# Two attention layers with routed and ternary feed-forward blocks on one core: attention loops issued in plan order, routing in eleven slot steps, LayerNorm roots and layer 1's normalization on GpSimd

## The chip, the cores and the metric

The kernel runs on one core of a Trainium2 chip. The metric is device microseconds (us) of one execution; lower is better. A core has TensorE (PE: matmuls, with weight loads, PEld, beside them), VectorE (DVE), ScalarE (ACT), GpSimd (POOL) and SyncE (SP, which issues most of the transfers here).

## The reference, cut to what matters

Eight sequences of 112 tokens and 256 features pass through two layers. Each block adds its result to x.

```python
x = x + xattn0(layernorm(x), ctx)      # 16 heads of 16, context of 375, biases
x = x + moe(layernorm(x))              # 8 experts of 256 -> 1024 -> 256, exact gelu, top 2
x = x + xattn1(layernorm(x), ctx, mask)
x = x + ffn(layernorm(x))              # ternary weights, 8-bit activations, depthwise conv, silu

def layernorm(x, eps=1e-5):
    return (x - mean(x)) / sqrt(var(x) + eps)
# routing: distances in a ball between x @ Wp + bp and 8 centroids,
# the two nearest experts, weights by softmax over -distance
```

## The kernel before, in words

All arithmetic on tokens is float32. x lies in SBUF as eight tiles of 112x256 (`xs`).

**Attention** (`attention(layer, ...)`, L479) works on one sequence ("batch" b) at a time and is laid out as a pipeline by a written plan. `add(slot, place, step, *args)` puts steps into the list `plan` (from L677); the loop at L741 calls them sorted by slot, then place, with ties in the order of adding. A batch starts every four slots, n = 4b. Its steps are: `norm` (normalize, two PE transposes t_n, ACT copy), `key` in two halves (t_k, evacuated by ACT), `value` (t_v, evacuated by DVE), `query` (t_q, scaled by DVE), then for the four head groups g `scores` (PE sc; DVE takes the row maximum, in layer 1 with the mask added), `lower` (transposes of the maxima, t_top; DVE adds them to the query as a 17th row), `turned` (transposed scores less the maximum, t_p; in layer 1 four DVE mask adds; two ACT exponentials), `weighted` (PE po), and at the end `finish_o` (ACT copy, PE t_o, DVE division), `finish_t` (PE t_oT, ACT copy) and `project` (PE t_out, DVE adds to x, then `ln_stats` for the next block).

PSUM holds three "pair" buffers of two banks, which sc (two of them), t_p (two), t_k and t_v (one each) take in turn; one "misc" bank, which t_n, t_q, t_top, t_o, t_oT, t_out, t_rn and t_xh take in turn; and one bank for po and the small products. A product waits until the engine that reads its buffer's last content is done.

`ln_stats` (L204) takes mean and variance, adds 1e-5 and calls `rsqrt` (L185): an integer first guess and three Newton steps, nine VectorE operations that wait for each other nearly all. `ln_apply` (L215) normalizes on VectorE.

In layer 0 the plan also holds the **routing** of the batches that are done (`Router`, L246, called by `route`), in eight steps from slot n+13 on: normalize and transpose (r_n, t_rn), products with Wp (t_xh), `centre` (products with the centroids and a DVE root), `distance`, two `pick`s, `place` (rank of each token by a product with a triangle, row numbers, two scatters of the normalized rows into `tok` in DRAM by GpSimd), and `weigh` (the two shares, a root of two columns). After it `further` works out which extra expert tiles there are. The ternary weights of the last block are made here as well (`ternary`, slots 8 to 19), and layer 1's keys and values of batches 0 and 1 (slots 31 to 45).

**Experts** (L756 on): 21 tiles of 128 rows are fetched from `tok`, pass through their expert with weights that come by transfers, and are written to `ysc` in DRAM. Layer 1's attention begins with `combine` (L506): two gathers of rows of `ysc` by GpSimd, two DVE multiply-adds into x, `ln_stats`. The **last block** quantizes and runs on bf16.

What an engine runs in which order is not given by the program's order: the framework's scheduler lists instructions by their priority (their place in the program) and by when it expects their inputs, engine by engine, and may put a later instruction ahead of an earlier one.

## Time and profile before

| | |
|---|---|
| median of the runs | 797.11 us (795.2 to 800.27) |
| the profiled execution, its own time | 795.12 us |
| its span, from the first to the last instruction | 793.4 us |
| mean granted TensorE clock | 0.841 |
| busy: PE, PEld, DVE, ACT, POOL | 670.2, 483.3, 462.1, 240.9, 43.3 us |
| attention 0 | 0 to 294 us |
| experts | 294 to 457 us |
| attention 1 | 457 to 700 us |
| last block | 700 to 793 us |

In the rows of slices each digit is the busy share of one fortieth of the span in tenths; the row PEclk has the granted clock in the same way. PE's records are modelled, so a busy PE includes products that run at half the clock and some of their waits. The table by windows gives, after the window's length, the busy time of each engine with the number of its instructions, then the clock, the share of the DMA engines and GB/s. The chain of waits leads back from the last instruction to what released it each time: start, length, engine, what it wrote, its line. A line of the timeline has start, length, engine, line, operation, output and input with shape.

### The profile page before, as it was taken

What the parts mean: (1) busy time and instruction counts of PE and PEld (TensorE: products, weight loads), DVE (VectorE), ACT (ScalarE), POOL (GpSimd) and SP (SyncE); (2) the same over time, 40 slices, a digit from 0 to 9 for tenths busy, and PEclk for the clock granted to TensorE, in tenths of its full rate; (3) what the DMA queues carried; (4) which work ended last, traced back from release to release, by engine and by line L of the source; (5) the groups of instructions that cost most, each with busy time, mean ns of one, the idle gap of its engine ahead of it and who ended that gap; (6) DMA issues with size and microseconds to landing.
All of it is one profiled execution on the core that took longest, in us unless ns stands there. A gap on an engine that the chain in (4) does not pass through costs nothing.

```text
span 793.4 us, 15060 instructions
## 1 busy us (share of the span) xinstructions
PE 670.2 (84%) x5906; PEld 483.3 (61%) x5906; DVE 462.1 (58%) x1664; ACT 240.9 (30%) x476; POOL 43.3 (5%) x83
## 2 busy tenths in 40 slices
PE   4999998999989819999999968999999989845143
PEld 2666666666656519998999844566666656621033
DVE  8853767766844760111111148759887785569975
ACT  1123342323233204434334310133433322317300
POOL 4000000100000110000000061000000000000000
PEclk9998999989777959999999975579999985556558
DMA  9999101002000115988899420000000000000001
GB/s 309 366 344 321 62 2 54 14 13 68 14 12 8 31 45 206 332 287 327 331 351 344 169 82 19 1 2 1 2 2 2 2 2 1 1 1 0 0 11 35
DMA packets 37074, 82.73 MB, mean 104 GB/s; under 512 B 3228, under 2 KB 29196, under 8 KB 31628
## 3 DMA queue, kind: packets, MB, share of 16 engines
q1 hardware_dynamic: 34092, 76.25, 27.2%
q0 software_dynamic: 1536, 3.67, 1.5%
q10 hardware_dynamic: 1376, 1.87, 0.7%
q8 instruction: 46, 0.75, 0.4%
q14 instruction: 24, 0.20, 0.1%
HBM read 61.59 MB, written 20.19 MB: 103 GB/s over the span
## 4 chain that ended last, share of the span: by engine, by line
PE 68%; DVE 20%; DMA 5%; issue 4%; ACT 3%; POOL 0%; another core or an unknown queue 0%; POOLq 0%; DVEq 0%; ACTq 0%; SPq 0%
PE t_k L229 10%; PE t_h L799 10%; PE t_y L810 9%; PE t_p L617 8%; PE sc L584 7%; PE po L639 6%; PE t_q L534 4%; PE t_v L236 4%; DMA tok<-rn,at 2%; DVE a L198 2%; PE t_out L672 2%; DVE am L924 2%; PE t_o L651 1%; DVE top L587 1%; PE t_y L942 1%
## 5 line engine op out<-in xcount | busy, mean ns | idle before, releaser
L229 PE MATMUL t_k<-ctx,wk 128*128 128x375 f32 x256 | 100.5, 538 | 4.0 <-DMA ctx<-in_ctxT_dram 3.2
L799 PE MATMUL t_h<-tnT,we 128*128 128x128 f32 x672 | 91.4, 280 | 0.6 <-DMA we<-in_WA_dram 0.4
L799 PEld LDWEIGHTS t_h<-tnT,we 128*128 128x128 f32 x672 | 87.1, 193 | 7.5 <-ACT hT L803 1.6
L584 PE MATMUL sc<-k,q 16*112 16x375 f32 x512 | 88.0, 593 | 4.3 <-DVE pT L627 3.2
L803 ACT ACTIVATE hT<-t_h,we 128x128 f32<-128x128 f32 x168 | 61.4, 368 | 91.3 <-PE t_h L799 85.7
L617 PE MATMUL t_p<-qa,k 17*125 17x112 f32 x1536 | 81.9, 323 | 2.4 <-DVE top L587 1.5
L810 PE MATMUL t_y<-we,hT 128*128 128x256 f32 x336 | 82.8, 380 | 0.0
L629 ACT ACTIVATE pT<-pT 125x672 f32<-125x672 f32 x64 | 48.8, 763 | 107.7 <-DVE pT L627 105.5
L617 PEld LDWEIGHTS t_p<-qa,k 17*125 17x125 f32 x1536 | 65.0, 215 | 21.2 <-issue 14.8
L587 DVE TENSOR_REDUCE top<-sc 112x2 f32<-112x750 f32 x64 | 57.9, 935 | 27.2 <-PE sc L584 27.2
L229 PEld LDWEIGHTS t_k<-ctx,wk 128*128 128x128 f32 x256 | 51.1, 211 | 37.1 <-issue 9.7
L627 DVE TENSOR_TENSOR pT<-t_p,maskT 125x336 f32<-125x336 f32 x128 | 56.6, 500 | 24.9 <-PE t_p L617 24.9
L639 PE MATMUL po<-pT,v 125*32 125x112 f32 x1536 | 65.9, 299 | 6.1 <-ACT pT L629 3.7
L629 ACT ACTIVATE pT<-t_p 125x672 f32<-125x672 f32 x64 | 43.3, 728 | 90.7 <-PE t_p L617 90.7
L594 DVE CUSTOM_DVE_ANT_0 sm<-sc,mask 112x375 f32<-112x375 f32 x128 | 63.1, 543 | 9.9 <-PE sc L584 9.9
L639 PEld LDWEIGHTS po<-pT,v 125*32 125x32 f32 x1536 | 43.4, 124 | 31.4 <-ACT pT L629 13.3
L810 PEld LDWEIGHTS t_y<-we,hT 128*128 128x128 f32 x336 | 59.1, 191 | 5.5
L788 DVE COPY tnT<-t_tn 128x256 f32<-128x256 f32 x21 | 8.9, 425 | 77.2 <-PE t_tn L786 70.6
L812 DVE TENSOR_TENSOR y<-t_y,we 128x256 f32<-128x256 f32 x21 | 8.9, 425 | 68.9 <-PE t_y L810 63.9
L584 PEld LDWEIGHTS sc<-k,q 16*112 16x112 f32 x512 | 29.4, 192 | 30.9 <-issue 19.7
L236 PE MATMUL t_v<-wv,ctx 128*125 128x256 f32 x192 | 45.9, 387 | 0.3 <-ACT k L557 0.3
L534 PEld LDWEIGHTS t_q<-nT,wq 128*128 128x128 f32 x256 | 36.2, 225 | 7.5 <-DVE qa L607 3.7
(207 smaller groups left out, 780.6 us busy)
## 6 DMA issues: line engine op xcount, KB each, us to landing
we<-in_WB_dram SPq DMA_DIRECT2D x21, 1152.0 KB, 8.2
we<-in_WA_dram SPq DMA_DIRECT2D x21, 1028.0 KB, 6.5
tok<-zero SPq DMA_DIRECT2D x8, 896.0 KB, 9.7
ysc<-zero SPq DMA_DIRECT2D x8, 896.0 KB, 10.8
ctx<-in_ctxT_dram SPq DMA_DIRECT2D x8, 375.0 KB, 6.5
tn<-tok SPq DMA_DIRECT2D x21, 128.0 KB, 7.4
ysc<-y SPq DMA_DIRECT2D x21, 128.0 KB, 3.3
we<-in_w1T_dram SPq DMA_DIRECT2D x1, 1024.0 KB, 9.4
```

What stands on the lines that cost most here:

```text
L229: nc.tensor.matmul(t, wts[layer]["k"][:, c, g * 128 : (g + 1) * 128], ctx_t[b][:, c, :], start=(c == 0), stop=(c == 1),)
L236: nc.tensor.matmul(t, ctx_t[b][:, c, i * KC : (i + 1) * KC], wts[layer]["v"][:, c, :], start=(c == 0), stop=(c == 1),)
L534: nc.tensor.matmul(t[:, g, :], wts[layer]["q"][:, c, g * 128 : (g + 1) * 128], nT[:, c, :], start=(c == 0), stop=(c == 1),)
L584: nc.tensor.matmul(ts[j // 2][:S, j % 2, :SK], q[r, g, :], k[r, g, :], start=True, stop=True)
L587: nc.vector.tensor_reduce(top[:, g, 2 * m : 2 * m + 2, A : A + 1], ts[m][:S, :, :SK], AX.X, ALU.max, negate=True,)
L594: nc.vector.tensor_tensor_reduce(out=sm, in0=ts[m][:S, i, :SK], in1=mask_t, scale=-1.0, scalar=3.0e38, op0=ALU.add, op1=ALU.min, accum_out ...
L617: nc.tensor.matmul(ts[j // 2][:KC, j % 2, c * S : (c + 1) * S], k[r, g, c * KC : (c + 1) * KC], qa[r, g, :], start=True, stop=True,)
L629: nc.scalar.activation(pT, src, AF.Exp)
L639: nc.tensor.matmul(po[32 * j : 32 * j + 32, g, :], v[:, c, 4 * g + j, :], pTs[j // 2][:, j % 2, c * S : (c + 1) * S], start=(c == 0), stop ...
L799: nc.tensor.matmul(ph[:, i, :], w1[:, c, f * 128 : (f + 1) * 128], nt[:, c, :], start=(c == 0), stop=(c == 1),)
L803: nc.scalar.activation(hT[:, f, :], ph[:, i, :], AF.Gelu, bias=b1[:, f : f + 1])
L810: nc.tensor.matmul(py, hT[:, f, :], w2[:, f, :], start=(f == 0), stop=(f == NF - 1))
```

## The change

The attention plans run inside `tc.manual_schedule` for PE, DVE, ACT and POOL: these four engines take the steps' instructions in the plan's order. SP isn't among them. The steps are divided further and moved:

- `combine`'s gathers become a step `gather`, three slots earlier; `combine` itself moves from place 0 to 5.
- `norm` is split: normalize at n-6, transposes (`norm_t`) at n-5. In layer 1, for b > 0, GpSimd normalizes.
- `finish_o`'s ACT copy becomes `finish_c` at n+9, place 8; `finish_o`, `finish_t` and `project` move from place 1 to 2.5, behind `weighted`.
- key, value and layer 1's early keys and values change places, the last three of them slots too.
- routing has eleven steps: the transposes, the root of `centre` (now `scale`) and the rank product of `place` (now `rank`) stand alone. Its normalized rows have three buffers in place of two.
- LayerNorm's root is two GpSimd operations, an add and a power of -0.5. The roots of the routing stay on VectorE.

```diff
+    minus_half = const([128, 1], "mhalf")
+    nc.gpsimd.memset(minus_half, -0.5)
...
         nc.vector.bn_aggr(mv, st)
-        nc.vector.tensor_scalar_add(mv[:, 1:2], mv[:, 1:2], 1e-5)
         rs = sp.tile([S, 1], F32, tag=f"rs{b}", name="rs")
-        rsqrt(mv[:, 1:2], rs, 1, "ln")
+        nc.gpsimd.tensor_scalar_add(rs, mv[:, 1:2], 1e-5)
+        nc.gpsimd.tensor_tensor(rs, rs, minus_half[:S], ALU.pow)
...
-    def ln_apply(dst, b, stats):
+    def ln_apply(dst, b, stats, eng=None):
         mv, rs = stats
-        nc.vector.tensor_scalar(dst, xs[b], mv[:, 0:1], rs, ALU.subtract, ALU.mult)
+        (eng or nc.vector).tensor_scalar(dst, xs[b], mv[:, 0:1], rs, ALU.subtract, ALU.mult)
...
-            g, r = tmp("g", E + 1), tmp("r", 1)
+            return t
+
+        def scale(self, t):
+            g, r = self.tmp("g", E + 1), self.tmp("r", 1)
             nc.vector.tensor_copy(g, t)
             self.ball_scale(g[:, E : E + 1], r, 1, "x")
             return g, r
...
+        def rank(self, b):
+
+            ind = self.ind
             t = self.small("t_rank")[:S, :E]
             nc.tensor.matmul(t, below[:S, :S], ind, start=True, stop=(b == 0))
             if b > 0:
                 nc.tensor.matmul(t, ones[:S, :S], count[(b - 1) % 2][:S], start=False, stop=True)
+            if b == 0:
+                nc.vector.tensor_copy(count[0][:S], ind)
+            else:
+                nc.vector.tensor_add(count[b % 2][:S], count[(b - 1) % 2][:S], ind)
+            return t
...
-            def combine(b):
-
+            def gather(b):
+
+                st[b]["y"] = []
                 for k in range(2):
                     y = ap3.tile([S, D], F32, tag=f"yg{k}", name="yg")
                     nc.gpsimd.indirect_dma_start(
...
+                    st[b]["y"].append(y)
+
+            def combine(b):
+                for k, y in enumerate(st[b].pop("y")):
                     nc.vector.scalar_tensor_tensor(xs[b], y, share[b][:, k : k + 1], xs[b], ALU.mult, ALU.add)
                 stats[b] = ln_stats(b)
 
             def norm(b):
                 n = ap.tile([S, D], F32, tag="n", name="n")
-                ln_apply(n, b, stats.pop(b))
+                ln_apply(n, b, stats.pop(b), nc.gpsimd if layer == 1 and b > 0 else nc.vector)
...
+            def finish_c(b):
+                st[b]["ou"] = ap.tile([128, G, S], F32, tag="ou", name="ou")
+                nc.scalar.copy(st[b]["ou"], st[b].pop("po"))
+
...
                 if layer == 1:
-                    add(n - 8, 0, combine, b)
-                add(n - 5, 6, norm, b)
+                    add(n - 11, 0, gather, b)
+                    add(n - 8, 5, combine, b)
+                add(n - 6, 6, norm, b)
+                add(n - 5, 6, norm_t, b)
                 if layer == 0 or b >= AHEAD:
 
                     ahead = layer == 1 and b == 2
-                    add(-7 if ahead else n - 4, 4, key, layer, b, 0)
-                    add(-7 if ahead else n - 3, 5, key, layer, b, 1)
-                    add(-7 if ahead else n - 2, 6, value, layer, b)
+                    add(-10 if ahead else n - 4, 4, key, layer, b, 0)
+                    add(-9 if ahead else n - 3, 4, key, layer, b, 1)
+                    add(-7 if ahead else n - 2, 4, value, layer, b)
                 add(n - 3, 2, query, b)
                 add(n + 4, 6, lower, b)
-                add(n + 10, 1, finish_o, b)
-                add(n + 11, 1, finish_t, b)
-                add(n + 12, 1, project, b)
+                add(n + 9, 8, finish_c, b)
+                add(n + 10, 2.5, finish_o, b)
+                add(n + 11, 2.5, finish_t, b)
+                add(n + 12, 2.5, project, b)
...
-                        r["n"] = rt.norm(b, stats_next.pop(b))
+                        r["n"] = rt.norm(b, stats_next.pop(b), ap3)
...
-                    for i in range(8):
-                        add(4 * b + 13 + i, 5 if i == 6 else 7, route, b, i)
+                    for i in range(11):
+                        add(4 * b + 13 + i, 7, route, b, i)
...
-                for b, ns in enumerate(((3, 6, 9), (15, 16, 17))):
-                    add(last + ns[0], 4, key, 1, b, 0)
-                    add(last + ns[1], 4, key, 1, b, 1)
-                    add(last + ns[2], 4, value, 1, b)
-
-            for slot, place, step, args in sorted(plan, key=lambda s: s[:2]):
-                step(*args)
-            if layer == 0:
-                res = rt.further()
+                for b, ns in enumerate(((3, 6, 9), (16, 18, 20))):
+                    add(last + ns[0], 8, key, 1, b, 0)
+                    add(last + ns[1], 8, key, 1, b, 1)
+                    add(last + ns[2], 8, value, 1, b)
+
+            ET = mybir.EngineType
+            with tc.manual_schedule(engines={ET.PE, ET.DVE, ET.Activation, ET.Pool}):
+                for slot, place, step, args in sorted(plan, key=lambda s: s[:2]):
+                    step(*args)
+                if layer == 0:
+                    res = rt.further()
```

Steps 0 to 10 of `route` are then: normalize, turn, hyper, centre, scale, distance, pick 0, pick 1, rank, place, weigh.

## The prediction

> **What bounds the kernel now.** I read, in order, the busy slices of the page, the table by windows, the chain of waits, and the timelines of four stretches. The profiled execution took 795.12 us, span 793.4. The page's slices (19.8 us each) show where TensorE (PE) is not full and where its granted clock falls:
>
> ```profile
> PE   4999998999989819999999968999999989845143
> ...
> DVE  8853767766844760111111148759887785569975
> ...
> PEclk9998999989777959999999975579999985556558
> ```
>
> PE is at 8 to 9 tenths in both attention loops, and its clock falls to 5 to 7 tenths in slices 11 to 13, 15, 24 to 27 and 34 to 39, counted from 1. By stage (attention 0, experts, attention 1, last block; columns: length, then PE, weight load, VectorE (DVE), ScalarE (ACT), GpSimd (POOL), clock):
>
> ```profile
> 0.00:294.00 294.00, 253.81 (x2512) 173.11 (x2512) 193.98 (x866) 84.70 (x165) 28.27 (x67) 0.89 0.33 111
> 294.00:457.00 163.00, 159.24 (x1053) 145.95 (x1054) 17.79 (x42) 62.72 (x169) 0.00 (x0) 0.98 0.79 288
> 457.00:700.00 243.00, 223.50 (x2214) 144.36 (x2213) 173.51 (x633) 70.08 (x101) 14.99 (x16) 0.78 0.03 9
> 700.00:793.00 93.00, 33.66 (x130) 19.92 (x129) 76.79 (x123) 23.36 (x41) 0.00 (x0) 0.60 0.03 10
> ```
>
> The experts are untouched. The loops leave 40 and 20 us of PE idle, and run at 0.89 and 0.78 of the clock. In the chain of waits the query product returns once a batch (start, length):
>
> ```profile
> 93.91 1.97 PE t_q L534 x16
> ...
> 121.56 3.60 PE t_q L534 x16
> ...
> 151.75 2.04 PE t_q L534 x16
> ...
> 181.71 2.04 PE t_q L534 x16
> ...
> 526.88 1.97 PE t_q L534 x16
> ...
> 551.07 1.97 PE t_q L534 x16
> ...
> 575.26 1.97 PE t_q L534 x16
> ```
>
> So a batch takes 27.65, 30.2 and 30.0 us in layer 0 while routing joins, but 24.2 us in layer 1 at full clock. The timeline of layer 1 (575 to 600 us) has PE without a gap and already in the plan's order, slot for slot. Issue in the plan's order therefore can't speed up the steady part; what it can change is the fill, the drain, and how VectorE's small operations mix. In a chain of dependent ones each starts 0.195 us after the one before:
>
> ```profile
> 240.11 0.16 DVE L202 SCALAR_TENSOR_TENSOR q<-a,q 112x2 f32<-112x2 f32 x1
> 240.31 0.16 DVE L200 TENSOR_TENSOR a<-q 112x2 f32<-112x2 f32 x1
> 240.50 0.16 DVE L201 SCALAR_TENSOR_TENSOR a<-a,z 112x2 f32<-112x2 f32 x1
> ```
>
> where the timeline at 145.8 to 146.5 us, two chains mixed, has starts 0.065 us apart. The order before mixes chains wherever it can; the plan's order runs one after the other.
>
> [...] during a GpSimd add at 17.22 us (0.73 us) a VectorE L202 took 0.65 us, not 0.15. [...] at 464 us (idle 7 us, then 0.50), but from 660 to 690 us PE is busy 29.2 of 30 us by the records at 0.50, so busy by the records isn't enough.
>
> **The change part by part.** Units: r0 to r3 are the slots 4b to 4b+3 of a batch; durations are from the timelines.
>
> *Start, +4.0.* The preamble and the plan's first slots now keep their order. Before, centroids ran mixed in and the first scores began at 24.08 us, the second query at 29.22. Now the centroid chain (16 dependent operations, about 3.2 us) stands after value 0's three adds (1.1) and batch 1's normalization (0.4), and before the first score reduction; its matmul stands before the first scores. From batch 0's normalization at 12.5 PE has t_n, t_k (5.0 with the starts of now), t_q 2.0, t_k and t_v 2.8 each: values end at about 25.6. Then csq is ready at 27.3, scores at 28, the chain ends at 31.4, the reduction that frees the pair buffer at 32.3; the second query then starts at 33.3.
>
> *Routed slots 13 to 31, +7.2.* Removed: ten root operations per batch from VectorE, mostly mixed into other chains, so worth about 0.1 us each, 1.0 us of a 30 us batch, which PE sets. Moved: the routing steps stand at place 7, behind value's adds and ahead of the next slot's reduction. From the end of a value product VectorE must now do, in order: adds 1.1, norm 0.4, place 0.85, distance (9 x 0.195) 1.75, reductions 1.8, weigh (16 x 0.195, plus) 3.3, pick 1.0, first reduction 0.93: 11.1 us before r0's t_p has its buffer. PE has turn, scores, po, t_oT, t_p, t_n, t_xh, scores, po, t_out: about 7.5. The rest of the batch on PE is t_p, t_k, t_top, t_g, scores, po, t_q, t_p, t_k, rank, scores, po, t_o, t_p, t_v: 18.6 by starts. So 29.8 us at full clock. Before, half-clock spells (142 to 148, 169 to 178 us) cost 1.7 and 3.4, mean 2.5, of its 30.0; I take 1.8 now, since part falls into the stall. 31.6 against 30.0, 4.5 batches.
>
> *Slots 31 to the experts, +2.5.* The order before wandered here: from the scores at 218.57 to batch 7's o at 264.62 it took 46.0 us, with t_p and po split in pieces (235 to 243) and turn waiting for a scatter to free its buffer (1.3 and 1.9 us). With three buffers and whole steps PE has about 33 us at full clock, 38.5 at 0.85 of it: -7.5. Then the drain is VectorE's: slots 38 to 50 hold, in order, two place, two distance, two weigh, five picks, two scales and so on, one chain after the other; by the durations above 33.1 us from o to batch 7's rows. Before, mixed, 264.62 to 288.1 (the cast): 23.4. +9.7, and 0.3 for PE's rank. Batch 1's t_k and t_v (8.4 us on PE), moved to slots 44 to 48, are hidden in this chain; without it they would cost 8.4. The two scatters behind the rows (5.7 us to the first expert load at 293.8) are the same.
>
> *Layer 1's start, -8.4.* The last y is done at 456.04. The gathers land as before (461.64, 462.82). Statistics end at 464.0. The root on GpSimd, add and power, appears nowhere in the trace: at least two memsets of 90 ns, at most two descriptor instructions of 0.95; I take 0.5. Value 2's copy (0.95) covers it up to 465.0. Normalize, transpose, copy, query at half clock: 470.3. Ahead of the query's scaling VectorE has combine 1, whose gathers now stand behind root 0 on GpSimd: issued 464.5 and 465.75, landing 2.85 later; scaling at 470.4. Batch 1's normalization stands on GpSimd behind root 1 and two gathers (2.5) and takes 0.3 (its memset of that size) to 0.73 (its two-input add); I take 0.7: 473.2. PE's transposes wait for it, the scores behind them: 474.0 against 479.78. Then six scores (1.6 at half clock), two queries (3.76), small transposes (2.3): first t_p at 493.7 against 500.64; VectorE is no longer behind, as it has combine 2 and 3 only, not 2 to 5 (1.6 and a 1.9 us root each). Then three slots of t_p, two mask adds, second exp, po: 1.54+1.85+0.8+1.15 = 5.4; the first key product at 511.5 against 519.87. Gathers three slots earlier are worth nothing in later batches: the data waited anyway. At 2 us instead of 0.5 a root would give back 3 us here.
>
> *Layer 1's steady part, +2.6.* Removed: the root's 1.9 us chain, which held the scores of r1 up (1.64 us where 0.90 is work): -0.75. Added: t_out now follows po, which waits for an exp, and no longer fills that wait: +0.75. finish_c's copy stands on ACT behind exp and key's evacuation (0.89+0.53), and po of r2 waits for it: PE has scores (0.83) ahead: +0.65. Four batches. GpSimd's normalization has a slot of slack. SP's queue isn't among the four ordered engines, and its transfers stand where they stood.
>
> *Layer 1's drain, +1.2* (t_o, t_oT, t_out now between po and t_p, one after the other; before, they lay in the waits), *last block, -1.0* (eight chained operations of batch 7).
>
> Sum: 4.0+7.2+2.5-8.4+2.6+1.2-1.0 = +8.1 us: 803.2 for the profiled execution. The median is 1.99 above it: 805.2.
>
> **Rivals.** (1) Faster, by the clock. At reduced clock attention 0 loses (20 to 270 us, window by window) about 25 us of PE time, attention 1 about 42. If even slots without wandering order keep the clock up and half of 67 returns, 8.1-33 gives 772; it decides from 8 us (an eighth), and below 0.99 from 16. For it: the clock falls at 464 with idle PE, and the wandering stretch 210 to 240 has 0.68. Against: 660 to 690 us has no heavy products, which the change leaves so. I would expect a quarter to a half, 772 to 789. (2) Much slower: the stalls of r3 halve the clock in each routed batch (3 us more, 13 in all) and in layer 1's steady part (24.2 us toward 28, 16 in all): 834. For it: spells at 142 and 169 us begin in just these slots. Against: layer 1's scores wait there already, at 1.00. (3) No difference: the steps behave as the order before, since PE's order hardly changes, and start and fill cancel: 797. Against: the serial drain is plain arithmetic. (4) That roots or normalization on GpSimd are not off the path (slow power, waits behind gathers): 3 to 8 us more; a part of my case's range.
>
> **How the numbers follow.** My case 0.47, own range 796 to 820 (root 0.2 to 2 us, half-clock 0 to 3 us a batch, drain mixed by halves); (1) 0.28; (2) 0.15; (3) 0.10. About 1% (789 to 805) is what a measurement of this kernel tells from no change. Slower: 0.28 of my 0.47, and (2): 0.43. Faster: (1) but 0.01: 0.27. Same: 0.19 of mine, 0.01 of (1), and (3): 0.30. The range leaves out 0.1 below, where (1) returns more than a third, and 0.1 above, most of (2): 781 to 832.
>
> **What would show it.** Right: a routed batch near 31 us with DVE the releaser of t_p; place, distance and weigh in unbroken 0.195 us steps; o of batch 7 to its cast near 33 us; layer 1's first t_p about 38 us after the last y (before 44.6); 24.8 us a batch. Wrong: a drain under 27 us, a clock above 0.85 in attention 1, or GpSimd roots above 1 us.

## The result and the profile after

The changed kernel takes 847.69 us (842.58 to 855.38, 4 runs) against 797.59 us before on the same chip: ratio 1.061, 95% interval 1.054 to 1.067. Slower by 6%, well above the forecast of 805.2 and its range. The profiled execution is the slowest of the four: 855.38 us, span 853.7, so its stages add up to 60.3 us more than before, some 10 more than the medians differ. The ratios and intervals in this document leave out executions that took over 1.5% more than the fastest of the same kernel (the profiled one is such a case); the medians hold all of them.

The page's rows of slices, now 21.3 us each:

```profile
PE   3799989889899872999999987999999998645233
...
DVE  4444555565666677010111015767777675359974
...
PEclk9798998796857856999999995579899885556558
```

PE is as full as before or nearly, VectorE a little less busy (449.6 us in place of 462.1), and the clock row has its low digits spread over the whole of attention 0 (slices 2, 8, 10, 12, 13, 15 and 16) instead of a few places. The table by windows at the new borders:

```profile
0.00:341.50 341.50, 276.13 (x2512) 188.68 (x2512) 198.26 (x706) 84.29 (x165) 41.84 (x100) 0.81 0.29 96
341.50:502.00 160.50, 159.11 (x1050) 145.53 (x1050) 17.81 (x42) 62.64 (x169) 0.00 (x0) 0.99 0.79 291
502.00:761.00 259.00, 228.25 (x2216) 146.62 (x2216) 157.36 (x478) 68.95 (x101) 36.70 (x53) 0.74 0.03 9
761.00:853.00 92.00, 32.34 (x128) 19.93 (x128) 76.20 (x113) 23.43 (x41) 0.87 (x2) 0.61 0.04 10
```

Attention 0 takes 47 us longer, at a clock of 0.81 in place of 0.89; attention 1 takes 16 us longer, at 0.74 in place of 0.78. The same products keep PE busy 22 and 5 us longer, which I put down to the lower clock; the rest is idle. The query products in the chain of waits give the batches:

```profile
140.16 1.97 PE t_q L553 x16
...
174.01 1.97 PE t_q L553 x16
...
212.10 1.97 PE t_q L553 x16
...
621.52 1.97 PE t_q L553 x16
...
647.85 1.97 PE t_q L553 x16
```

33.8 and 38.1 us a batch in layer 0 (before 27.7 to 30.2), 26.3 us in layer 1 (28.3 in the batches between; before 24.2).

Cutting each profiled execution at the same events (VectorE's addition of a batch's t_out to x, "out 0" to "out 7"; the first expert's first product; the last y) gives the table that the rest refers to. The three columns on the right are experiments ("last version" is the last one of them).

| us | before | changed | no order by hand | all repairs | last version |
|---|---|---|---|---|---|
| start to out 0 | 88.4 | 103.2 | 88.4 | 91.5 | 92.5 |
| out 0 to 4 (routed batches) | 114.8 | 135.5 | 124.1 | 108.9 | 109.4 |
| out 4 to 7 | 67.6 | 63.1 | 60.7 | 67.2 | 54.8 |
| out 7 to first expert product | 25.3 | 39.8 | 26.5 | 39.1 | 26.6 |
| experts | 159.6 | 160.1 | 160.4 | 160.0 | 159.7 |
| last y to layer 1's out 0 | 88.9 | 86.1 | 88.0 | 86.2 | 83.4 |
| out 0 to 4 | 96.6 | 108.8 | 109.5 | 105.1 | 95.1 |
| out 4 to 7 | 59.7 | 64.4 | 59.0 | 52.9 | 51.8 |
| last block | 92.5 | 92.8 | 91.8 | 93.1 | 92.7 |

Each column is one execution. Some experiments keep the changed kernel's order of instructions in one layer, so that their traces measure that part again: out 0 to 4 took 131.5 to 139.4 us in five traces of layer 0 and 102.0 to 108.8 us in four of layer 1. Both ranges lie above the kernel before, whose own trace has 114.8 and 96.6, but a difference of a few microseconds between two columns can be the execution's.

Three places in the trace show where it goes. **The start**, by the timeline:

```profile
27.75 0.35 DVE L783 TENSOR_SCALAR mask<-mask 112x375 f32<-112x375 f32 x1 [7.10 <-DMA mask<-in_mask_dram]
...
29.32 0.34 DVE L784 TENSOR_SCALAR maskT<-maskT 125x336 f32<-125x336 f32 x1 [1.22 <-DMA maskT<-in_maskT_dram]
...
31.12 0.61 PE L543 MATMUL t_n<-ident,n 112*128 112x112 f32 x2 [6.00 <-DVE csq L270]
...
32.34 1.60 PE L603 MATMUL sc<-k,q 16*112 16x375 f32 x8
```

Two scalings of the masks, which only layer 1 reads and which stand behind attention 0 in the program, are outside the part ordered by hand, and the scheduler put them ahead of value 0's additions. There VectorE waits for the masks' transfers with all of the start behind it; before, the same two ran at 33.79 and 34.06 us, and neither waited. The brackets hold the idle time before an instruction and what ended it.

**A routed batch**, while the scores of batch 5 run, from value's additions to t_p's wait:

```profile
187.06 1.09 DVE L590 TENSOR_TENSOR v<-t_v,rows 125x256 f32<-125x256 f32 x3 [2.33 <-PE t_v L239]
...
188.38 0.16 DVE L382 TENSOR_TENSOR row<-po,first 112x8 f32<-112x8 f32 x1
...
189.69 0.21 DVE L330 SCALAR_TENSOR_TENSOR xn<-g,r 112x1 f32<-112x1 f32 x1
...
191.77 1.78 DVE L606 TENSOR_REDUCE top<-sc 112x2 f32<-112x750 f32 x2
...
192.75 1.60 PE L636 MATMUL t_p<-qa,k 17*125 17x112 f32 x20 [2.63 <-DVE top L606]
```

Between the additions and the reductions VectorE normalizes and does place (188.38) and distance (189.69), and t_p waits 2.63 us for its buffer. Two stretches of the batch before, at its wait and behind it (length, busy PE, PEld, DVE, ACT, POOL, clock):

```profile
154.70:157.80 3.10, 0.04 (x2) 0.00 (x0) 2.82 (x14) 0.01 (x1) 0.72 (x1) 0.99 0.01 3
157.80:169.00 11.20, 10.39 (x91) 7.12 (x92) 5.61 (x12) 2.91 (x8) 0.15 (x1) 0.54 0.27 95
```

3.1 us without a product, and then 11 us at 0.54 of the clock, which cost more than the wait did (10.39 us busy, times the 0.46 that the clock lacks, is 4.8).

**A batch of layer 1**:

```profile
637.32 1.59 ACT L648 ACTIVATE pT<-pT 125x672 f32<-125x672 f32 x2 [1.59 <-DVE pT L646]
...
638.96 1.31 PE L658 MATMUL po<-pT,v 125*32 125x112 f32 x20 [0.39 <-ACT pT L648]
...
640.20 2.05 PE L694 MATMUL t_out<-wo,oT 128*112 128x256 f32 x4
```

po waits 0.39 us for an exponential, and t_out behind it runs at half clock (2.05 us; 1.12 in the kernel before at 1.00, at 567, 591, 615 and 639 us).

### The profile page after: what moved, and what is told of

It reads as the page before. It is cut to its first block, busy times and chain, and to the rows that moved or that the text cites. A ratio compares the mean times of both kernels' runs of the same rounds, so it can differ in the third digit from the quotient of the medians.

```text
span 853.7 us, 14773 instructions
## 1 busy us (share of the span) xinstructions
PE 695.8 (82%) x5906; PEld 500.8 (59%) x5906; DVE 449.6 (53%) x1337; ACT 239.3 (28%) x476; POOL 79.4 (9%) x155
## 3 DMA queue, kind: packets, MB, share of 16 engines
q1 hardware_dynamic: 34092, 76.25, 25.2%
## 4 chain that ended last, share of the span: by engine, by line
PE 67%; DVE 17%; ACT 5%; DMA 5%; issue 4%; POOL 1%; SPq 1%; ACTq 0%; DVEq 0%; POOLq 0%
PE t_k L232 10%; PE t_h L831 9%; PE t_p L636 9%; PE t_y L842 8%; PE po L658 6%; PE sc L603 5%; PE t_v L239 4%; PE t_q L553 4%; PE t_out L694 3%; ACT pT L648 3%; DVE am L956 1%; PE t_xh L300 1%; PE t_y L974 1%; DVE y L945 1%; PE t_o L673 1%
## 5 line engine op out<-in xcount | busy, mean ns | idle before, releaser
L232 PE MATMUL t_k<-ctx,wk 128*128 128x375 f32 x256 | 110.1, 583 | 0.5 <-DVE y L844 0.5
L831 PE MATMUL t_h<-tnT,we 128*128 128x128 f32 x672 | 91.8, 281 | 0.9 <-DMA we<-in_WA_dram 0.7
L658 PE MATMUL po<-pT,v 125*32 125x112 f32 x1536 | 69.5, 310 | 25.5 <-ACT pT L648 12.5
L636 PE MATMUL t_p<-qa,k 17*125 17x112 f32 x1536 | 81.4, 342 | 10.4 <-DVE top L606 10.4
L835 ACT ACTIVATE hT<-t_h,we 128x128 f32<-128x128 f32 x168 | 61.4, 367 | 91.8 <-PE t_h L831 86.1
L648 ACT ACTIVATE pT<-pT 125x672 f32<-125x672 f32 x64 | 48.7, 763 | 135.3 <-DVE pT L646 132.9
L658 PEld LDWEIGHTS po<-pT,v 125*32 125x32 f32 x1536 | 46.1, 128 | 69.0 <-ACT pT L648 25.7
L603 PE MATMUL sc<-k,q 16*112 16x375 f32 x512 | 84.6, 616 | 0.6 <-DVE top L613 0.5
L636 PEld LDWEIGHTS t_p<-qa,k 17*125 17x125 f32 x1536 | 66.4, 236 | 30.3 <-issue 14.8
L232 PEld LDWEIGHTS t_k<-ctx,wk 128*128 128x128 f32 x256 | 56.6, 232 | 39.4 <-issue 18.9
L646 DVE TENSOR_TENSOR pT<-t_p,maskT 125x336 f32<-125x336 f32 x128 | 56.0, 500 | 23.6 <-PE t_p L636 23.5
L239 PEld LDWEIGHTS t_v<-wv,ctx 128*125 128x125 f32 x192 | 35.0, 187 | 7.4 <-ACT k L576 0.9
```

The lines of the kernel that those rows point to most:

```text
L232: nc.tensor.matmul(t, wts[layer]["k"][:, c, g * 128 : (g + 1) * 128], ctx_t[b][:, c, :], start=(c == 0), stop=(c == 1),)
L239: nc.tensor.matmul(t, ctx_t[b][:, c, i * KC : (i + 1) * KC], wts[layer]["v"][:, c, :], start=(c == 0), stop=(c == 1),)
L603: nc.tensor.matmul(ts[j // 2][:S, j % 2, :SK], q[r, g, :], k[r, g, :], start=True, stop=True)
L636: nc.tensor.matmul(ts[j // 2][:KC, j % 2, c * S : (c + 1) * S], k[r, g, c * KC : (c + 1) * KC], qa[r, g, :], start=True, stop=True,)
L646: nc.vector.tensor_tensor(pT[:, i, :], src[:, i, :], maskT_t, ALU.add)
L648: nc.scalar.activation(pT, src, AF.Exp)
```

## The experiments

All times are medians of device time against the kernel before on the same chip; bases differ by chip (793 to 798 us). Where an interval stands, it is that of the ratio to the kernel before, from three or more executions.

### Whose order is it?

**No order by hand** (the changed plan, ordered by the scheduler).

```diff
-            with tc.manual_schedule(engines={ET.PE, ET.DVE, ET.Activation, ET.Pool}):
+            if True:
```

> The changed kernel with its plan, steps and GpSimd roots as they are, but the planner's scheduler orders all engines again (no order by hand). Theory A (the frozen issue order is the cause: VectorE's in-order chains and waits stall TensorE, and the stalls halve its clock): most of the 50 us comes back, 797 +-10 us; a routed batch in layer 0 at 30 us or less, layer 1 at 24.2 us a batch, about 24 us from the last batch's output product to the first expert load (39.8 in the changed kernel). Rival B (what the plan itself moves is the cause: t_out behind po, the copy on ScalarE behind the exponentials, eleven routing steps, roots and normalization on GpSimd): 830 to 850 us.

811.1 us, with executions from 793.5 to 821.6. So by the medians 37 of the 50 us belong to the order by hand (26 to 54 by its slowest and fastest execution), and the plan's own part is about 14, with a spread that reaches to nothing. The table's third column says which is which: start and drain are as before, but the routed batches (31.0 us each) and layer 1's batches (27.4) are not, in this one execution. Neither theory alone: A missed the batches, B the start and the drain.

**VectorE left to the scheduler**, the other three by hand.

> The changed kernel with the order by hand on TensorE, ScalarE and GpSimd only; VectorE's order is the scheduler's. Theory A1 (it is VectorE's frozen order): 805 to 815 us, since TensorE's waits for top go, and the start and the drain come back. Rival A2 (TensorE's and ScalarE's frozen order): above 835 us.

843.0 us (ratio 1.057, 1.052 to 1.061). A1 falls. First scores are at 27.5 us and the drain is 31.7 us, so VectorE's own order matters in those two, but routed batches take 32.7 us and layer 1's 28.7: TensorE still waits in the plan's order for a VectorE that now does other things first (t_p 3.9 us for value's additions, which cost it nothing in the changed kernel).

**The mask scalings at slot 12.**

```diff
+                add(12, 9, nc.vector.tensor_scalar_mul, mask_t, mask_t, 0.0625)
+                add(12, 9, nc.vector.tensor_scalar_mul, maskT_t, maskT_t, 0.0625)
...
-    nc.vector.tensor_scalar_mul(mask_t, mask_t, 0.0625)
-    nc.vector.tensor_scalar_mul(maskT_t, maskT_t, 0.0625)
```

> The changed kernel with the two scalings of the masks (needed in layer 1 only) put into the plan at slot 12, place 9; in the changed kernel they stand in VectorE's queue ahead of the first value's adds, 7.1 and 1.2 us in wait for the masks' transfers. Theory A: the first scores start near 27.5 us instead of 32.4 and the clock is not halved from 28 to 38 us; together 9 to 10 us: 838 us. Rival: the centroid chain in front of the first reductions costs that time and the masks hide behind it: 844 to 848 us.

843.2 us (1.059, 1.053 to 1.065); executions 837.2 to 849.9. In the trace the start is what the theory says: first scores at 26.8 instead of 32.3 us, out 0 at 91.7 instead of 103.2, the only wait left there 1.6 us for csq. In the medians it is 4.5 us, and the intervals overlap, so its size at the end of the kernel is not settled by this run. The start itself is: it took 100.9 to 103.2 us in the six traces that have the changed kernel's start, and 91.5 to 96.4 in the seven with the scalings at slot 12 (six of these have other places moved too).

**The order by hand on the kernel before**, its own plan and steps.

> The kernel before with its own plan, steps and VectorE roots, but with the order by hand on TensorE, VectorE, ScalarE and GpSimd. Theory A: as slow as the changed kernel or slower, 845 to 875 us, since its routing steps are coarser (product and read of it in one step) and the roots' chains stay on VectorE. Rival B: 797 to 815 us.

901.8 us (1.129, 1.125 to 1.132). The order by hand costs the old plan 104 us and the changed plan about 37. In that order the rest of the change wins back 54 us, which I had not seen at all; 28 to 33 of them are the move to GpSimd, by the run further down that takes it back, so 21 to 26 are left for the finer steps and moved places. The direction is theory A's, the size is not.

### Layer 1's batches

**t_out at place 1**, ahead of po.

```diff
-                add(n + 12, 2.5, project, b)
+                add(n + 12, 1 if layer == 1 else 2.5, project, b)
```

> The changed kernel with layer 1's output product at place 1 again, ahead of po, as in the kernel before; all else as changed, order by hand included. In the changed kernel layer 1 takes 26.3 and 28.3 us a batch in turn, with 0.57 and 0.39 us of stall and a spell at half clock from t_out on. Theory C (the output product behind po leaves a run of some 6 us of small products without a large one, ending in po's stall, after which the clock halves): 24.8 us a batch, clock 1.00 there, the drain shorter too; 835 us. Rival D (the place doesn't matter, the half-clock spells come from ScalarE's copy or from GpSimd's work): 844 to 850 us.

847.9 us (1.069, 1.064 to 1.074), 27.0 us a batch: theory C fails as put. All these products share one bank, and t_out now waits 0.94 us for the copy of n's transpose, which stands on ScalarE behind an exponential. The stall moved and the clock stayed: 0.91 from out 0 to 4, as in the changed kernel.

**Filling products**, in that place: once t_out itself (128 rows), once two products of 16 rows and the same 256 columns.

```diff
+            def fill(b):
+                t = misc("t_out")[:S, :D]
+                st[b]["t_out"] = t
+                if b + 3 < B:
+                    ...          # two products into t
+                add(n + 12, 1, fill, b)
```

> The changed kernel with a further run of layer 1's output product for batches 0 to 4, ahead of po, into the bank that the real product then overwrites (work that changes no result). It fills po's 0.39 us stall with a product of 128 rows. Theory C and its like: the clock stays at 1.00 from batch 3 to 7 and a batch takes 25.6 us each (24.9 plus 1.1 less 0.4). Rival (the clock falls for another reason): 26.9 and 29 us.

> The same filling in the same place and of the same columns, but with products of 16 of 128 rows (scores' operands), so about the same 1.1 us of TensorE time and the same stall filled. If the stall (idle time) halves the clock: as with the large product, 25.6 us a batch at 1.00. If it is the run of small products: the spells stay or grow, 27 to 29 us a batch.

One execution each: 857.6 and 872.7 us. Both fillings met the same new stall of 0.94 us for the bank (beside the 0.57 us for po's copy), so the first did not do what I expected. But between the two only the rows differ, and out 0 to 4 reads, with the large product

```profile
587.90:700.10 112.20, 106.97 (x1159) 69.85 (x1161) 77.95 (x237) 35.03 (x51) 13.29 (x21) 0.91 0.02 6
```

and with the small one

```profile
593.10:714.20 121.10, 115.73 (x1154) 74.88 (x1158) 78.57 (x237) 35.27 (x51) 13.29 (x21) 0.84 0.02 5
```

Same stalls, clock 0.84 against 0.91, 8.9 us in four batches. That points to the rows, but doesn't show it by itself: these are one execution each, and traces with one and the same order in this stretch differ by up to 0.08 in the clock. The part on why the prediction was wrong comes back to it with all traces.

**ScalarE's copies early**: three places.

```diff
-                add(n - 5, 6, norm_t, b)
+                add(n - 5, 2.2 if layer == 1 else 6, norm_t, b)
-                add(n + 9, 8, finish_c, b)
+                add(n + 9, 2.1 if layer == 1 else 8, finish_c, b)
-                add(n + 12, 2.5, project, b)
+                add(n + 12, 1 if layer == 1 else 2.5, project, b)
```

> The changed kernel with three places of layer 1 moved so that ScalarE's copies don't stand behind an exponential that waits: the copy of po (finish_c) at 2.1 instead of 8, the transpose of n at 2.2 instead of 6, the output product at 1 instead of 2.5. Theory G (the stalls of 0.57 and 0.39 or 0.94 us, all behind ScalarE's copies, start the half-clock spells): no stall and 24.3 us a batch at 1.00, layer 1 some 14 us shorter, 833 us. Rival (the run of small products starts the spells without a stall): 26 us a batch or more, 842 to 850 us.

833.2 us (1.047, 1.039 to 1.054): theory G's size, but not for its reason alone. The stalls behind ScalarE are gone, and two others stand there: t_oT 0.44 us for the copy of n's transpose (one bank again), scores 0.55 us for VectorE's mask additions. Out 0 to 4 takes 100.7 us, 25.2 a batch, not 24.3; the drain is 5 us shorter as well (59.1 against 64.4).

### Routing

**weigh one slot later.**

```diff
-                        add(4 * b + 13 + i, 7, route, b, i)
+                        add(4 * b + 13 + i + (i == 10), 7, route, b, i)
```

> The changed kernel with routing's last step (weigh, 16 dependent VectorE operations, 3.3 us) one slot later, in r0 instead of r3 of a batch. Theory (VectorE's work between the end of the value product and the first reduction of r0 is what t_p waits for, 3.08, 2.63 and 2.18 us in batches 4 to 6, and the clock halves behind it): the waits fall below 0.5 us, a routed batch from 34 to 30 to 31 us, 834 us in all. Rival (the waits only move to another t_p, VectorE being full in every slot): 844 to 852 us.

859.0 us (1.080, 1.076 to 1.083), slower. t_p waits 3.07, 2.62 and 2.18 us, the same as in the changed kernel, so the theory falls. Weigh was never in front of it, and later it only lengthens the rest: out 4 to the first expert product takes 112.7 us (102.9 in the changed kernel). The lines of batch 5 above show what stands in front (in batch 4 a weight conversion of 1.22 us takes place's position).

**Routing and conversions ahead of the large product** (place 3.5 and 3.6).

```diff
-                    add(8 + i, 5, step)
+                    add(8 + i, 3.6, step)
-                        add(4 * b + 13 + i, 7, route, b, i)
+                        add(4 * b + 13 + i, 3.5, route, b, i)
```

> The changed kernel with the routing steps at place 3.5 instead of 7 and the weight conversions of the last block (ternary steps) at 3.6 instead of 5: ahead of the slot's key or value product instead of behind it, so that VectorE does them while TensorE is in that product. Theory F (t_p waits 2.2 to 3.1 us a batch because the conversion, norm, place and distance stand between value's adds and the next slot's reductions; moving weigh alone changed none of it): the waits fall below 1 us, a routed batch from 33.9 to 30.5 us, 833 us in all. Rival (TensorE now waits for routing's small products in front of its large ones instead): 848 to 860 us.

833.3 us (1.047, 1.041 to 1.054). The total is theory F's; the way there is only half of it. t_p's waits in the routed batches are gone but for one of 1.30 us, yet t_n now waits 1.23 us a batch for ScalarE, and the profiled execution, the slowest of four at 842.6, has 32.1 us a batch.

### Together

**All repairs**: the mask scalings, early routing, ScalarE's copies and t_out early in both layers, and, once no scores are left, t_p ahead of po.

```diff
-                    add(n + 5 + g, 3, turned, b, g)
+                    add(n + 5 + g, 3 if n + 5 + g < 4 * B else 1.5, turned, b, g)
```

> The order by hand on all four engines, with every repair at once: mask scalings at slot 12, routing and conversions ahead of the large product, ScalarE's copies and the output product early in both layers, t_p ahead of po once no scores are left. If the stalls named so far are the whole cause, the sum is 847 less 10 (start), 14 (routed batches), 14 (layer 1's steady part) and 5 (its drain): 804 us. If the order by hand has a cost of its own, whatever the places: above 820 us.

805.3 us (1.013, 1.005 to 1.022). The sum of the parts was 804; that the total meets it is luck, since the parts don't. Against the changed kernel's trace the routed batches gain 26.6 us where 14 were summed, layer 1's steady part 3.7 where 14 were, its drain 11.5 where 5 were. Routed batches now take 27.2 us, less than before (28.7), with TensorE's waits for VectorE and for ScalarE shorter together: from out 0 to 4 t_p waits 1.1 us for the reductions (10.0 in the changed kernel), and TensorE 3.4 us for ScalarE (5.9). Out 0 to 4 with early routing alone:

```profile
102.90:231.30 128.40, 120.03 (x1230) 80.94 (x1228) 77.89 (x233) 38.93 (x79) 10.36 (x15) 0.84 0.10 33
```

and with all repairs:

```profile
91.50:200.40 108.90, 102.46 (x1254) 70.57 (x1246) 77.63 (x235) 39.33 (x79) 10.35 (x15) 0.98 0.12 38
```

VectorE and ScalarE do the same work in both; the clock is 0.98 instead of 0.84, and of the 19.5 us PE's busy time gives 17.6.

**Layer 0 by the scheduler, layer 1 by hand with ScalarE's copies early**, and t_p ahead of po in its drain.

> Layer 0 in the scheduler's order (as in the run without order by hand), layer 1 in the order by hand with the three places of the run before this one, and the exponent products t_p ahead of po once no scores are left. Theory: layer 0 as without order by hand (first expert load near 298 us), layer 1 at 24.3 us a batch and 242 us from the last y to its end: 797 us. Rival (layer 1's order by hand keeps its stalls): 808 to 815 us.

793.1 us against 793.1 (1.000, 0.997 to 1.002, twelve executions); 797 was expected. From out 0 to 4 its layer 0 has the order of the run without order by hand, instruction for instruction, but took 132.9 us in this trace (the slowest of the twelve) and 124.1 in that one.

**The order by hand given up in layer 0's drain**, from slot 32 or 38 on, with all repairs.

```diff
+            end = 32 if layer == 0 else 99
...
+                for slot, place, step, args in plan:
+                    if slot < end:
+                        step(*args)
+            for slot, place, step, args in plan:
+                if slot >= end:
+                    step(*args)
```

> The kernel with every repair, but the order by hand in layer 0 ends at slot 32, after the last scores; what is left of layer 0 (its drain: 7 finishing groups and four batches' routing) is ordered by the scheduler. If VectorE's unmixed chains are what makes the drain long: the first expert load near 294 us instead of 304 to 306, 795 us in all. If the drain's length is the later start of routing in the plan (11 steps instead of 8): no gain, 803 to 807 us.

> The same, with the order by hand until slot 38 (the exponent and output products of the drain too, but not the routing chains behind them). If only the chains behind batch 6's o matter: like the run before, 795 us. If the backlog of routing that is built up in slots 32 to 38 matters: between, 799 to 803 us.

778.8 us (0.978, 0.973 to 0.984) and 783.0 us (0.985, 0.979 to 0.990): both faster than the kernel before. The stretch from out 7 to the first expert product, in the changed kernel:

```profile
301.70:341.50 39.80, 17.73 (x61) 12.68 (x61) 29.47 (x174) 3.20 (x7) 6.56 (x8) 0.63 0.10 30
```

and with the order given up at slot 32:

```profile
261.70:288.20 26.50, 7.96 (x42) 6.31 (x42) 19.10 (x149) 1.43 (x5) 6.56 (x8) 0.62 0.15 47
```

PE is mostly idle in both. VectorE has 25 operations fewer left there and is busy for 10.4 us less, and the stretch is 13.3 us shorter; all repairs without the cut had left it at 39.1. So the drain's cost is the order, as predicted, and not the later start of routing, which is the same in all of these. That it is VectorE's order above all is shown by the run that freed VectorE alone (from batch 7's o to its rows 30.6 us, 37.6 in the changed kernel, 26.0 with the cut at 32). The gain is larger than expected, since out 4 to 7 shrinks as well, from 67.2 to 54.8 us (63.2 with the cut at 38).

**Layer 1's transposes moved too** (all repairs, order by hand to the end).

```diff
-                add(n - 6, 6, norm, b)
-                add(n - 5, 2.2, norm_t, b)
+                add(n - 6 - layer, 6, norm, b)
+                add(*((n - 6, 6) if layer == 1 else (n - 5, 2.2)), norm_t, b)
-                add(n + 11, 2.5, finish_t, b)
+                add(n + 11, 1 if layer == 1 else 2.5, finish_t, b)
```

> The kernel with every repair, and in layer 1 normalization and transpose of n one slot earlier (the transpose behind the value product) and the transpose of o at place 1, so that neither stall left there (0.44 us for the copy of n's transpose, 0.55 us for VectorE's mask additions) should arise. If these stalls start the half-clock spells: 24.2 us a batch at 1.00 in each execution, 797 us. If not: spells in most batches as now, 803 to 807 us.

795.7 us (1.001, 0.996 to 1.006), 9.6 less than without. No wait of PE over 0.25 us is left between outs 0 and 4, and a batch takes 23.6 us, less than the 24.2 before. Out 0 to 4 with all repairs:

```profile
552.80:657.90 105.10, 102.00 (x1138) 66.42 (x1134) 77.82 (x238) 36.05 (x51) 13.29 (x21) 0.91 0.02 6
```

and with the transposes moved (1.00 until 644 us; then the drain begins, and the clock is 0.50 from 646 to 662 us, with PE busy for all of it):

```profile
552.80:647.80 95.00, 94.36 (x1126) 62.15 (x1118) 77.72 (x238) 36.07 (x51) 13.29 (x21) 0.98 0.02 7
```

In this pair of traces two stalls of together 1 us a batch cost 10 us in four batches, 2.5 of them as idle time. But TensorE's order of all repairs stands in five traces, which took 97.5 to 105.1 us here, and the order with the transposes moved in three, which took 95.0 or 95.1. So the stalls cost 2.5 to 10 us, by the execution, and without them the time hardly varied. The moved places also changed which products stand next to each other, so the stalls are not the only difference between the two orders.

**Roots and layer 1's normalization back on VectorE**, all else as changed.

> The changed kernel with the LayerNorm roots (ten operations, 1.9 us in one chain) and layer 1's normalization back on VectorE; order by hand, plan and steps as changed. If GpSimd's part is on the path (my rival 4): 3 to 8 us faster than the changed kernel, 840 to 845 us; the second query's transpose in layer 1's start waits 2.5 us less. If VectorE's queue is what matters: slower, since every root then stands in front of a reduction, 852 to 862 us.

875.8 us (1.102, 1.096 to 1.109): 28 us slower than the changed kernel by the medians, 33 by the ratios. Rival 4 falls. GpSimd's pair takes 0.81 us, and with it a chain of 1.9 us is out of VectorE's order.

**Both**: order given up at slot 32 in layer 0, transposes moved; and then layer 1's order given up at slot 32 as well.

> The kernel with every repair, layer 0's order by hand given up at slot 32 (778.8 us) and layer 1's transposes moved as in the run that had 23.6 us a batch. If the two add: 778.8 less 8 to 10 us, 770 us. If the gain in layer 1 shows only behind the long drain: 776 to 780 us.

> The same with layer 1's order by hand given up at slot 32 too. If the order by hand costs something in layer 1's drain as it does in layer 0's: 2 to 4 us less than the run before this one. If that drain is bound by t_p, exponential and po in a chain that VectorE's other work doesn't touch: the same within 1 us.

776.4 us (0.970, 0.964 to 0.975) and 768.8 us (0.961, 0.957 to 0.966) against 797.3. The first is in between: as a ratio 0.9 points below the 0.978 without the moved transposes (they gave 1.2 where the drain was long), with overlapping intervals. In the second, layer 1's drain itself is the same within 1 us (51.8 us from out 4 to 7); of the 5.3 us between the two profiled spans 4.7 lie ahead of the experts, where the order of instructions is the same in both traces, so I don't ascribe the further gain to the edit. 768.8 us is the best version, 3.9% below the kernel before by the ratio.

## Why the prediction was wrong

Sign right, size wrong: +8.1 predicted, +60.3 in the profiled execution. The steps that failed most are the half-clock time behind short stalls (1.8 us a batch in the routed slots, less than before, and nothing in layer 1's steady part) and the start, which left out what the scheduler does outside the ordered part; these three terms are 34 of the 52 us that were missing. Term by term, in the order of the sum:

| term | predicted | profiled |
|---|---|---|
| start | +4.0 | +14.8 |
| routed slots | +7.2 | +20.7 |
| slots 31 to the experts | +2.5 | +10.1 |
| layer 1's start | -8.4 | -2.8 |
| layer 1's steady part | +2.6 | +12.2 |
| layer 1's drain | +1.2 | +4.7 |
| last block, experts | -1.0 | +0.8 |

- **Start.** The centroid chain in front of the first reductions was right, and the times nearly so once the masks are out of the way (csq ready at 26.1 in that run, 27.3 predicted; first scores at 26.8, 28 predicted). The 10 us on top are the mask scalings. I had asked whether SP's transfers stay where they stood, but not what the scheduler does with instructions outside the ordered part.
- **Routed slots.** The mechanism holds: DVE releases t_p, and place and distance run in steps of 0.2 us behind the value's additions. The wait's size, 3.6 us by 11.1 less 7.5, compares with 3.08, 2.63 and 2.18; but I put it before r0's t_p with weigh in its list, and it is one slot earlier, at r3's, with weigh behind it. That the sizes are near each other is luck. The term that failed is "I take 1.8 now, since part falls into the stall": half clock (busy time times what the clock lacks) costs 4.9 us a batch (19.4 us of PE time in four; 2.1 a batch before; 4.0 to 6.1 in the five traces with this order). The stall doesn't absorb the half-clock spell: with all repairs, where idle time is back at 6.4 us, half clock costs 0.4 us a batch. With early routing alone, at 8.4 us idle, it still cost 5.0, so the two don't fall in step. This was rival 2's mechanism, and with 834 us rival 2 came nearest. I had counted against it that layer 1's scores wait at full clock. Idle time and half clock together (in stretches of 2 us) grew from 14.4 to 36.0 us over these four batches, beside the 20.7 us of the table.
- **Slots 31 to the experts.** -4.5 where I had -7.5 for the wandering order, +14.6 for 10.0 in the drain. The chains from o to batch 7's rows took 37.6 us by the timeline (33.1 predicted, 23.4 before): right in kind and shown by the runs cut at slots 32 and 38. Another 2.3 us came behind the rows, where weigh's chain stands in front of `further`, which the first expert load waits for; I had called that part the same.
- **Layer 1's start.** The last y to the first scores 20.0 us (18.0 predicted, 23.7 before), to the first t_p 40.4 (37.7), to batch 3's first key product 58.6 (55.5, before 63.8). Of the two sizes that I had only bounded, the root is inside its bounds but above what I took, and the normalization is above its upper bound. The groups of GpSimd's operations (total, mean ns, idle before):

```profile
L215 POOL TENSOR_TENSOR rs<-rs,mhalf 112x1 f32<-112x1 f32 x32 | 17.8, 563 | 2.0
L220 POOL TENSOR_SCALAR n<-x,mv,rs 112x256 f32<-112x256 f32 x7 | 8.7, 1244 | 0.4
L214 POOL TENSOR_SCALAR rs<-mv 112x1 f32<-112x1 f32 x32 | 8.0, 251 | 289.4 <-DVE mv L212 277.5 <-DVE m L353 11.8
```

  A root takes 0.81 us where I took 0.5, and a normalization 1.24 where I took 0.7 with 0.73 as the bound: the second batch's transpose waits 5.77 us for it, behind the root and two gathers. The rest of the term, some 2.4 us between batch 3's first key product and out 0, is not explained here.
- **Layer 1's steady part.** The stalls were right: 0.57 us behind finish_c's copy (0.65 predicted), 0.39 behind the exponential (0.75). That half-clock spells follow the latter was not in the sum. 97 us at 1.00 became 109 us at 0.91 (102.0 to 108.8 at 0.97 to 0.91 in the four traces with this order).
- **Layer 1's drain.** Its idle time grew from 7 to 17 us (668 to 761 us against 617 to 701): the copy of po behind the next exponential (3.48 us once) and po behind the exponential of the slot before (1.93 or 1.94 us, four times). With t_p ahead of po and the copy early, it takes 52.9 us, less than before. I had judged the drain's order by PE's products alone.
- **The claim that the plan's order can't speed up the steady part** was wrong too: with no stall left, a hand-ordered layer 1 runs at 23.6 us a batch against 24.2.

**What the clock did.** In layer 1 of the changed kernel each of four stalls of 0.39 us ahead of po was followed by a spell at half clock, from 611.73, 639.03, 666.34 and 693.65 us, of 3.41 or 6.83 us. In all twenty traces the granted clock is 1 or 0.5, and its changes lie multiples of 3.413 us apart (27 changes in the trace before and 43 in the changed kernel's, all within 0.01 us of multiples of 3.4133), so a spell lasts 3.4, 6.8 or 10.2 us or more. Counted from the span's start, the changes lie 2.29 us behind a multiple in the trace before and 0.74 in the changed kernel's, so which products share a step differs by execution. Here are three steps of layer 1 with all repairs, then three with the cut at slot 38: the same products in the same order with the same two stalls (0.44 and 0.55 us), and TensorE is busy for the same times, but the clock falls in the first and not in the second.

```profile
572.42:575.84 3.42, 2.98 (x43) 1.58 (x45) 2.79 (x9) 1.17 (x3) 0.00 (x0) 1.00 0.00 0
575.84:579.25 3.41, 2.86 (x35) 1.65 (x36) 2.59 (x9) 1.76 (x3) 0.00 (x0) 1.00 0.02 5
579.25:582.66 3.41, 3.41 (x51) 2.33 (x49) 2.02 (x9) 0.06 (x1) 0.80 (x2) 0.50 0.01 2
...
554.52:557.93 3.41, 2.97 (x60) 1.87 (x56) 2.58 (x11) 0.69 (x2) 0.00 (x0) 1.00 0.00 0
557.93:561.34 3.41, 2.86 (x41) 1.68 (x41) 3.41 (x13) 1.52 (x2) 0.00 (x0) 1.00 0.02 7
561.34:564.76 3.42, 3.42 (x34) 2.25 (x31) 3.28 (x9) 1.53 (x2) 0.80 (x2) 1.00 0.00 0
```

So the times that TensorE was busy and idle do not tell these two apart. In the step after which the clock falls there are mostly scores and t_p, products of 16 and 17 rows; in the second execution the whole of t_out, with 128 rows, lies in the step with the second stall. As a measure of my own, weight TensorE's time in a step by the rows of its products (the 17 in t_p's 17*125), divided by 128: the step before the fall has 0.28 of its length, the two of the other execution 0.45 and 0.55. In the attention parts of all traces, none of 130 steps at full clock with a weighted share below 0.3 was followed by full clock, but 1271 of 1283 with 0.6 or more were. Of the steps at half clock in which TensorE was busy for 97% or more, 1 of 477 with a share below 0.7 was followed by full clock, and 232 of 248 with 0.8 or more. The two fillings fit: the steps at half clock in which the first four of each stood had 0.82 to 0.91 with 128 rows, and three were followed by full clock; with 16 rows they had 0.42 to 0.52, and none was.

What decides in between stays open. The counts come from runs made for other ends, between these shares either clock can follow (346 of 513 steps at full clock between 0.3 and 0.6 kept it), and whether a product's columns count too was not settled. Executions of one kernel differ by up to 28 us; that the place of the steps makes this difference was not shown.

## What to carry to other kernels

When an order is frozen, price every short stall on TensorE twice: once as idle time, and again as half-clock time that may follow it, in these traces mostly where the weighted share of a step was below 0.6. Here the second grew by about as much as the first in the routed batches (11.2 us beside 10.4), and in layer 1's steady part it was 3 to 10 us by the execution, beside 4. In a frozen order each slot's reader has its own deadline: list for each buffer what stands between its last write and its release on the releasing engine, slot by slot, including ScalarE's copies behind an exponential that itself waits. Freeze the steady loop only, leave fills and drains made of small dependent chains to a scheduler that mixes them, and look where instructions outside the frozen part end up.

## What the runs showed that I had not expected

- GpSimd's operations on a 112x1 column cost 0.25 us (add) and 0.56 us (power), and a 112x256 normalization with two scalars per row 1.24 us, three times VectorE's 0.41. Moving them off VectorE was still worth 28 to 33 us in the order by hand.
- The granted clock was 1 or 0.5 in all traces and changed only at moments that lie multiples of 3.413 us apart; counted from the span's start they lay 2.29 us behind a multiple in one trace and 0.74 in another. Steps at full clock with a weighted share of 0.6 or more were followed by full clock in 1271 of 1283 cases, those below 0.3 in none of 130. The same stalls of 0.44 and 0.55 us in the same order of instructions were followed by half clock in one execution and by full clock in another.
- A difference of a few microseconds between two traces can be the execution's: one order of TensorE's instructions took 97.5 to 105.1 us in layer 1's four batches.
